# A graph network on one core: the back of a batch as one stream, and as two that overlap

## The chip, the cores and the metric

One core of a Trainium2 chip runs the whole program. The metric is the time of one execution on the device, in microseconds (us); the runs' median is given. The core's engines work side by side, each through its own queue of instructions in the order of the program: TensorE (PE in the profile, its weight loads PEld), VectorE (DVE), ScalarE (ACT), GpSimd (POOL) and SyncE (SP, which here only issues DMAs).

## The reference

16 graphs of 1024 nodes with 64 channels, and a dense weighted adjacency of which some 1.6% is not zero. Four layers, each x = layernorm(x + f(x)):

```python
# layer 0: GCN
x = ln(x + adj @ (x @ w0) + b0)
# layer 1: quantiles over neighbours
adj_ = where(eye, 1, adj)                       # self loops
nb = (adj_ > 0) & ~eye;  m = nb.sum(-1)         # degree
rank = cumsum(nb) - 1
skip = where(m > 10, (m + 1) // 2, 1)
removed = nb & (skip > 1) & mask & ((rank + 1) % skip == 0)
valid = where(removed | removed.T, 0, adj_) > 0
agg = 0.25 * q25 + 0.5 * q50 + 0.25 * q75       # over x[valid neighbours], per channel
x = ln(x + (relu((x + agg) @ W1 + b1) @ W2 + b2) * mask)
# layer 2: three rounds of message passing
h = x @ We
for i in range(3): h = relu(adj @ (h @ Wl[i] + bl[i]))
x = ln(x + (h @ Wp + bp) * mask)
# layer 3
t = adj @ x
x = ln(x + where(t > 0.5, 1, 0))
```

## The kernel before

A batch (one graph) goes through five kinds of work, each written as a Python generator that emits some instructions and yields their cost in planned steps:

- `words_of`: the adjacency comes in eight rows of tiles (`arow`, L488), is transposed on PE, goes to DRAM for later (`adjd`, L604), gives layer 0, and is packed into words of neighbour bits.
- `front` with `listing`: nodes are ranked by their number of neighbours, so that tiles of nodes with similar lists are sorted together. One-hot matrices `perm` (L730, DVE) carry the words into rank order on PE (L735, L736) into PSUM banks "wd", ACT copies them out (L772, L773), and DVE makes lists of neighbours from them (first `bit`, L780). It ends with a table of x1 in DRAM.
- per group of tiles (five groups, `GROUPS`): `gathered` fetches the neighbours' rows by indirect DMAs from POOL (L933; 122 and 7 packed ones a batch), `masked` spoils what does not count (`hits` L981 on DVE, L988 on ACT), `quantiles` runs a sorting network on DVE (L1038) between the buffers `g` and `s`, and `summed` weights the rows on ACT (L1074) and adds them on PE (L1067).
- `back`: the rest of layer 1 and the layers 2 and 3. `to_nodes` brings the sums from rank order back to node order: each of three bf16 `pieces` of the sums is multiplied on PE (L1122) with one-hot matrices `ones_at`, which ACT makes in two operations of 1024 columns (L1117, L1118; in the last batch five of eight are made by DVE, L1114), into two banks at once. Then x1 is added (L1128), two small matmuls and a `residual` with layernorm give x2; the adjacency is read back (`adjB`, L1271, 4 MB); three layers of matmuls with it (L1339, L1350) and a residual give x3; one more aggregation (`aggregate`, L445), a comparison (L1365) and a layernorm give y, which is stored (L1369).

The order of all instructions is made before the program runs. A heap holds the generators by due time; the earliest emits its next step, and its due time grows by the yielded cost times its stretch. `LENGTHS` are the planned durations of the five groups, 192.06 in sum; `start(q)` is the planned start of group q. `back` is due 1.2 after its batch's last group, polls until all five sums are in and the batch before is `done`, and its stretch is BACK / BACK_STEPS = 178/181. One `back` is emitted before the next begins. A gather is also made to follow the fifth DVE and the fourth ACT instruction before it in this order (`follow`). `words_of` of a batch polls until the batch four before is `done` (`LIVES`), and `front` polls until its words are there.

Rooms: PSUM has eight banks: "mm" 2, "tp" 2, "wd" 2, "ax" 1, "agg" 1. In SBUF the one-hot tiles of all kinds (`nb`, `perm`, `ones_at`, `back_to`) share seven rooms of the tag "onehot", and `s` has two rooms. `ENDS` says in which buffer a sorted row ends (1 is `s`).

## Time and profile before

| | |
|---|---|
| median of 10 runs | 3122.62 us (3117.95 to 3126.34) |
| the profiled execution's own time | 3116.19 us |
| its span, first to last instruction | 3114.4 us |
| granted TensorE clock, mean | 0.878 of full speed |
| start of the second subtraction of pieces (L1107), batches 3 to 11 | 871.2, 1049.1, 1227.2, 1404.6, 1584.4, 1763.1, 1942.0, 2121.9, 2299.0 us |

```
## 2 busy tenths in 40 slices
PE   6534697888979798897969788896978889685777
PEld 5434454545545454554545454554545455343443
DVE  7388998989999999999899899989999999987741
ACT  2344757567676756667576756767575666747531
POOL 0577777777777777777777777777777777777600
```

Each digit of a slice row is the busy share of one of 40 equal slices of the span in tenths (9 is 90% or more). In lines of waits the numbers are the total, the count and the longest, in us. In a timeline a line begins with start and duration, and the bracket says how long the engine was idle before and which instruction ended that. In windows an engine's number is its busy time in the stretch, with the instructions in brackets; the last three are the granted clock, the DMA engines' share and GB/s.

### The profile page before, as it was taken

What the parts mean: (1) busy time and instruction counts of PE and PEld (TensorE: products, weight loads), DVE (VectorE), ACT (ScalarE), POOL (GpSimd) and SP (SyncE); (2) the same over time, 40 slices, a digit from 0 to 9 for tenths busy, and PEclk for the clock granted to TensorE, in tenths of its full rate; (3) what the DMA queues carried; (4) which work ended last, traced back from release to release, by engine and by line L of the source; (5) the groups of instructions that cost most, each with busy time, mean ns of one, the idle gap of its engine ahead of it and who ended that gap; (6) DMA issues with size and microseconds to landing.
All of it is one profiled execution on the core that took longest, in us unless ns stands there. A gap on an engine that the chain in (4) does not pass through costs nothing.

```text
span 3114.4 us, 49256 instructions
## 1 busy us (share of the span) xinstructions
PE 2461.5 (79%) x13893; PEld 1508.2 (48%) x13894; DVE 2708.4 (87%) x7852; ACT 1890.4 (61%) x6153; POOL 2207.5 (71%) x2078
## 2 busy tenths in 40 slices
PE   6534697888979798897969788896978889685777
PEld 5434454545545454554545454554545455343443
DVE  7388998989999999999899899989999999987741
ACT  2344757567676756667576756767575666747531
POOL 0577777777777777777777777777777777777600
PEclk8667798989989898998989899898989899787879
DMA  2433334433243434324343433434333332313110
GB/s 87 112 91 77 72 83 116 103 99 103 72 130 93 117 97 116 90 62 147 77 120 90 116 103 83 113 78 128 90 115 101 102 97 71 84 30 85 22 58 5
DMA packets 169079, 282.74 MB, mean 91 GB/s; under 512 B 99485, under 2 KB 102112, under 8 KB 166880
## 3 DMA queue, kind: packets, MB, share of 16 engines
q1 hardware_dynamic: 67584, 142.01, 13.6%
q0 software_dynamic: 66048, 69.88, 13.6%
q10 hardware_dynamic: 35168, 67.62, 5.9%
q8 instruction: 115, 1.88, 0.3%
q14 instruction: 164, 1.34, 0.1%
HBM read 204.33 MB, written 71.44 MB: 89 GB/s over the span
## 4 chain that ended last, share of the span: by engine, by line
DVE 21%; PE 16%; ACT 8%; DMA 3%; issue 2%; POOL 0%; DVEq 0%; POOLq 0%; ACTq 0%
PE mm L1350 8%; DVE s L1038 6%; DVE g L1038 6%; DMA g<-table,idx 3%; ACT ones_at L1117 2%; PE ax L535 2%; ACT g L988 2%; ACT ones_at L1118 2%; PE mm L445 1%; ACT g L1074 1%; PE pa L1067 1%; DVE top L796 1%; PE mm L1339 1%; DVE cand L800 1%; PE tp L510 1%
## 5 line engine op out<-in xcount | busy, mean ns | idle before, releaser
L933 POOL DMA_INDIRECT g<-table,idx x1952 | 2088.0, 1070 | 704.1 <-DMA g<-table,idx 144.4
L1350 PE MATMUL mm<-adjB,msg 128*128 128x512 f32 x1536 | 753.8, 612 | 9.6 <-ACT msg L1342 9.6
L988 ACT ACTIVATE g<-g,bias 128x64 f32<-128x64 f32 (+9 forms) x2272 | 598.1, 339 | 223.8 <-DVE bias L984 164.6
L1038 DVE TENSOR_TENSOR s<-g 128x384 f32<-128x384 f32 (+8 forms) x1200 | 575.8, 495 | 10.2 <-ACT at L512 0.5
L1038 DVE TENSOR_TENSOR g<-s 128x256 f32<-128x256 f32 (+10 forms) x1040 | 501.5, 500 | 3.7
L1067 PE MATMUL pa<-g,ident 128*128 128x128 f32 (+1 forms) x1600 | 332.2, 328 | 117.3 <-ACT g L1074 115.1
L1074 ACT ACTIVATE g<-g,w 128x64 f32<-128x64 f32 x1552 | 394.0, 336 | 29.0 <-DVE w L1045 28.6
L1067 PEld LDWEIGHTS pa<-g,ident 128*128 128x128 f32 x1600 | 269.3, 219 | 266.1 <-ACT g L1074 186.9
L1350 PEld LDWEIGHTS mm<-adjB,msg 128*128 128x128 f32 x1536 | 265.3, 194 | 200.5 <-issue 176.9
L1122 PE MATMUL mm<-ones_at,pieces 128*64 128x512 bf16 x768 | 217.7, 428 | 130.7 <-ACT ones_at L1118 130.7
L535 PE MATMUL ax<-at,xt 128*64 128x128 f32 x1920 | 271.1, 301 | 0.0
L535 PEld LDWEIGHTS ax<-at,xt 128*64 128x64 f32 x1920 | 241.1, 154 | 57.4 <-issue 54.3
L445 PE MATMUL mm<-adjB,x 128*64 128x512 f32 x512 | 245.4, 613 | 8.9 <-DVE x L482 8.9
L1038 DVE TENSOR_TENSOR g<-g 128x256 f32<-128x256 f32 (+7 forms) x432 | 213.2, 507 | 2.5
L1038 DVE TENSOR_TENSOR g<-g,s 128x256 f32<-128x256 f32 (+5 forms) x512 | 209.3, 414 | 3.2
L1122 PEld LDWEIGHTS <-pieces 128*64 128x64 bf16 x768 | 90.1, 120 | 218.8 <-issue 162.2
L510 PE MATMUL tp<-ident,arow 128*128 128x128 f32 x1024 | 165.5, 291 | 24.8 <-DMA arow<-in_adj_dram 16.3
L1353 ACT ACTIVATE hlT<-mm 128x512 f32<-128x512 f32 x96 | 57.2, 596 | 206.2 <-PE mm L1350 206.2
L510 PEld LDWEIGHTS tp<-ident,arow 128*128 128x128 f32 x1024 | 128.0, 150 | 88.0 <-issue 65.4
L735 PE MATMUL wd<-hi,perm 128*128 128x55 f16 x960 | 84.3, 206 | 108.5 <-DVE perm L730 108.3
L981 DVE TENSOR_SCALAR hits<-g,nself 128x38 f32<-128x38 f32 (+4 forms) x128 | 31.6, 247 | 146.6 <-DMA g<-table,idx 122.7
L1010 ACT ACTIVATE hat<-iota,npos 128x10 f32<-128x10 f16 (+2 forms) x384 | 114.4, 298 | 68.7 <-DVE npos L997 67.6
(228 smaller groups left out, 4030.9 us busy)
## 6 DMA issues: line engine op xcount, KB each, us to landing
arow<-in_adj_dram SPq DMA_DIRECT2D x128, 512.0 KB
adjd<-at ACTq DMA_DIRECT2D x120, 512.0 KB
adjB<-adjd SPq DMA_DIRECT2D x15, 4096.0 KB
g<-table,idx POOLq DMA_INDIRECT x1952
table<-xc ACTq DMA_DIRECT2D x16, 264.0 KB
xt<-in_x_dram SPq DMA_DIRECT2D x16, 256.0 KB
out_dram<-y SPq DMA_DIRECT2D x16, 256.0 KB
stage<-table,packed POOLq DMA_INDIRECT x112
```

The costliest lines, as they stand in the source:

```text
L445: nc.tensor.matmul(pa[:C, :], src[:, m, :], adjT[:, h * TH:(h + 1) * TH, m, :], start=(m == 0), stop=(m == T - 1))
L510: nc.tensor.transpose(pt[:, i * P:(i + 1) * P], a[:, j * P:(j + 1) * P], ident)
L535: nc.tensor.matmul(self.bank[:C, cols], self.xt[:, m + 1, :], at[:, m, :], start=(m == 0), stop=(m == T - 1))
L735: nc.tensor.matmul(pw[:, :hn], ws, hi[:, t, :], start=False, stop=False)
L933: g = nc.gpsimd.indirect_dma_start(out=dst, out_offset=None, in_=st["table"], in_offset=bass.IndirectOffsetOnAxis(ap=index, axis=0))
L988: nc.scalar.activation(v, v, AF.Identity, bias=bias[:m, i, k:k + 1])
L1010: nc.scalar.activation(h, iota[:, lo:lo + kw], AF.Abs, bias=npos[:, i, s:s + 1])
L1038: vector.tensor_tensor(box(bufs[mode >> 1 & 1], d, run, sd, count, tile), box(bufs[mode >> 3], a, run, sa, count, tile), box(bufs[mode >> ...
L1067: nc.tensor.matmul(pa[:, :(e - k) * nt * C], ident, rows_.rearrange("p (k c) -> p k c", c=R)[:, :, :C], start=(j == 0), stop=(j == len(run ...
L1074: nc.scalar.activation(slots(g, bufs[0], lo + r, lo + r + 1)[:, i, 0, :C], slots(g, bufs[at[r]], lo + r, lo + r + 1)[:, i, 0, :C], AF.Iden ...
L1122: nc.tensor.matmul(bank[:C, :], pieces[:, i, s, :], ones_at[:, h * HALF:(h + 1) * HALF], start=(s == 0 and i == 0), stop=False)
L1350: nc.tensor.matmul(pg, msg[:, m, :], adjT[:, h * TH:(h + 1) * TH, m, :], start=(m == 0), stop=(m == T - 1))
```

## The change

The `back` becomes two generators. `back_one` goes to x2, with its own rooms for channels, hidden layer, pieces and layernorm, and one PSUM bank of its own, "one"; the bank comes from "wd", of which one is left, so that the permuted words of a batch lie in one bank (8 x 55 columns) and are copied out at once. `back_two` does the rest; it is due 70 planned units after `back_one`, and waits for x2 of its batch and `done` of the batch before. `back_one` waits for x2 of the batch before, no longer for `done`. So the two of neighbouring batches can stand side by side in the order. Inside `to_nodes` the nodes are done in two halves, one after the other, each with `ones_at` of 512 columns and one bank. "onehot" has six rooms for seven and `s` one for two; the sorting network of 13 ends all rows in `g` (one operation of 256 columns becomes two of 128). Other generators keep their due times; the read of `adjB` stands at the start of `back_two`.

```diff
@@ -51,8 +51,8 @@
 LIVES = 4
 STATE = ("nself", "kept", "minus")
 LENGTHS = (50.06, 35, 54.5, 19.5, 33)
-WORDS, LISTS, BACK = 152.6, 133.2, 178
-WORDS_STEPS, LISTS_STEPS, BACK_STEPS = 82.0, 74.0, 181.0
+WORDS, LISTS, BACK1, BACK2 = 152.6, 133.2, 70.0, 160.0
+WORDS_STEPS, LISTS_STEPS, BACK1_STEPS, BACK2_STEPS = 82.0, 74.0, 67.0, 134.0
 BEFORE = 7.874
 AFTER = 1.2
...
@@ -162,7 +162,7 @@
...
-    13: "1000000000",
+    13: "0000000000",
...
@@ -414,7 +414,10 @@
         return psum("tp", 2)
 
     def psum_wd():
-        return psum("wd", 2)
+        return psum("wd", 1)
+
+    def psum_one():
+        return psum("one", 1)
 
     def psum_ax():
         return psum("ax", 1)
@@ -427,10 +430,10 @@
 
 
 
-    def to_channels(dst, src):
+    def to_channels(dst, src, bank):
 
         for h in range(NH):
-            pt = psum_mm()
+            pt = bank()
             for i in range(TH):
                 nc.tensor.transpose(pt[:C, i * P:(i + 1) * P], src[:, h * TH + i, :], ident)
             yield 1.5
...
@@ -723,18 +726,17 @@
         yield 0.4
 
         hn = W + NEXT
-        pws = [psum_wd() for _ in range(NH)]
-        for pw in pws:
-            nc.tensor.matmul(pw[:, :TH * hn], zeros, iota[:, :TH * hn], start=True, stop=False)
+        pws = psum_wd()[:, :T * hn]
+        nc.tensor.matmul(pws, zeros, iota[:, :T * hn], start=True, stop=False)
         def one_hot(t, perm):
             vector.tensor_scalar(perm, iota, rank[:, t:t + 1], None, op0=ALU.is_equal)
 
         def permuted(t, s, perm):
-            pw = pws[s // TH][:, (s % TH) * hn:]
+            pw = pws[:, s * hn:(s + 1) * hn]
             ws = perm[:, s * P:(s + 1) * P]
-            nc.tensor.matmul(pw[:, :hn], ws, hi[:, t, :], start=False, stop=False)
+            nc.tensor.matmul(pw, ws, hi[:, t, :], start=False, stop=False)
             nc.tensor.matmul(pw[:, :W], ws, lo[:, t, 1:W + 1], start=False,
-                             stop=(t == T - 1 and s % TH == TH - 1))
+                             stop=(t == T - 1 and s == T - 1))
 
         if st["b"] == 0:
...
@@ -766,13 +768,11 @@
                     yield 1.0
             st["permuted"] = True
         for half in halves:
-            for h2 in sorted({s // TH for s in half}):
-                v = pws[h2][:, :TH * hn].rearrange("p (t k) -> p t k", k=hn)
-                ts = slice(h2 * TH, (h2 + 1) * TH)
-                nc.scalar.copy(wd[:, ts, :], v[:, :, :W])
-                nc.scalar.copy(num[:, ts, :], v[:, :, W:])
-                yield 0.8
             ts = slice(half[0], half[-1] + 1)
+            v = pws.rearrange("p (t k) -> p t k", k=hn)[:, ts, :]
+            nc.scalar.copy(wd[:, ts, :], v[:, :, :W])
+            nc.scalar.copy(num[:, ts, :], v[:, :, W:])
+            yield 1.2
             wi = wd[:, ts, :]
             for r in range(ROUNDS):
                 if r + 1 < ROUNDS:
...
@@ -1020,7 +1020,7 @@
         nt = len(tiles)
         while ("hat", g) not in st:
             yield 0.5
-        bufs = st["g", g], srt.tile([P, KMAX * R], F32, tag="y", name="s", bufs=2)
+        bufs = st["g", g], srt.tile([P, KMAX * R], F32, tag="y", name="s", bufs=1)
 
         def box(buf, first, run, step, count, tile):
             v = buf[:, (first * nt + max(tile, 0)) * R:]
...
@@ -1099,7 +1099,7 @@
 
 
         ag = st["ag"]
-        pieces = act.tile([P, S, T, C], BF16, tag="msg", name="pieces")
+        pieces = act.tile([P, S, T, C], BF16, tag="pieces", name="pieces")
         for i in range(S):
             nc.scalar.copy(pieces[:, i], ag)
             yield 0.8
@@ -1107,29 +1107,29 @@
                 vector.tensor_tensor(ag, ag, pieces[:, i], ALU.subtract)
                 yield 0.8
         st["moved"] = True
-        banks = [psum_mm() for _ in range(NH)]
-        for s in range(T):
-            ones_at = tmp.tile([P, N], BF16, tag="onehot", name="ones_at", bufs=7)
-            if st["b"] == B - 1 and s % 3:
-                vector.tensor_scalar(ones_at, iota, st["minus"][:, s:s + 1], 0.0,
-                                        op0=ALU.add, op1=ALU.is_equal)
-            else:
-                nc.scalar.activation(ones_at, iota, AF.Abs, bias=st["minus"][:, s:s + 1])
-                nc.scalar.activation(ones_at, ones_at, AF.Relu, bias=1.0, scale=-1.0)
-            yield 1.9
-            for h, bank in enumerate(banks):
+        for h in range(NH):
+            cols = slice(h * HALF, (h + 1) * HALF)
+            bank = psum_one()
+            for s in range(T):
+                ones_at = tmp.tile([P, HALF], BF16, tag="onehot", name="ones_at", bufs=6)
+                if st["b"] == B - 1 and s % 3:
+                    vector.tensor_scalar(ones_at, iota[:, cols], st["minus"][:, s:s + 1], 0.0,
+                                            op0=ALU.add, op1=ALU.is_equal)
+                else:
+                    nc.scalar.activation(ones_at, iota[:, cols], AF.Abs, bias=st["minus"][:, s:s + 1])
+                    nc.scalar.activation(ones_at, ones_at, AF.Relu, bias=1.0, scale=-1.0)
+                yield 1.0
                 for i in range(S):
-                    nc.tensor.matmul(bank[:C, :], pieces[:, i, s, :],
-                                     ones_at[:, h * HALF:(h + 1) * HALF],
+                    nc.tensor.matmul(bank[:C, :], pieces[:, i, s, :], ones_at,
                                      start=(s == 0 and i == 0), stop=False)
-            yield 1.7
-        for h, bank in enumerate(banks):
+                yield 0.9
             for i in range(TH):
                 nc.tensor.matmul(bank[:C, i * P:(i + 1) * P], st["x1"][:, h * TH + i, :], ident,
                                  start=False, stop=(i == TH - 1))
             yield 1.2
-            nc.scalar.copy(dst[:, h * HALF:(h + 1) * HALF], bank[:C, :])
-        yield 1.0
+            nc.scalar.copy(dst[:, cols], bank[:C, :])
+            yield 0.6
...
@@ -1262,65 +1262,66 @@
         return st
 
 
-    def back(st):
-        b, x1 = st["b"], st["x1"]
-        while "words" in st and (st.get("sums", 0) < len(GROUPS) or "done" not in st["before"]):
+    def residual(src, w_sb, first, base, y, mb, bank, who):
+
+        py = bank()
+        add_bias(py, first, C, T)
+        for t in range(T):
+            nc.tensor.matmul(py[:, t * C:(t + 1) * C], src[:, t * P:(t + 1) * P], w_sb,
+                             start=False, stop=(t == T - 1))
+            if t % 2:
+                yield 1.0
+        yield 1.0
+        u = act.tile([P, T, C], F32, tag="u" + who, name="u")
+        vector.tensor_tensor(u, nodes(py), spread(mb, C), ALU.mult)
+        yield 0.7
+        vector.tensor_tensor(u, u, base, ALU.add)
+        yield 0.7
+        yield from layernorm(u, y, who)
+
+    def node_tile(name, tag, bufs=1):
+        return act.tile([P, T, C], F32, tag=tag, name=name, bufs=bufs)
+
+    def back_one(st):
+        x1 = st["x1"]
+        while "words" in st and (st.get("sums", 0) < len(GROUPS) or "x2" not in st["before"]):
             yield 0.5
+        oT = act.tile([C, N], F32, tag="chan1", name="oT")
+        if "agg" in st:
+            o = act.tile([P, T, C], F32, tag="ua", name="o")
+            vector.tensor_tensor(o, x1, st["agg"], ALU.add)
+            yield 0.7
+            yield from to_channels(oT, o, psum_one)
+        else:
+            yield from to_nodes(oT, st)
+        hT = act.tile([H, N], F32, tag="hT1", name="hT")
+        for h in range(NH):
+            cols = slice(h * HALF, (h + 1) * HALF)
+            ph = psum_one()
+            nc.tensor.matmul(ph, w1_sb, oT[:, cols], start=True, stop=True)
+            yield 1.3
+            nc.scalar.activation(hT[:, cols], ph, AF.Relu, bias=b1_sb)
+            yield 0.7
+        x2 = node_tile("x2", "x2", 2)
+        yield from residual(hT, w2_sb, C, x1, x2, st["mb"], psum_one, "a")
+        st["x2"] = x2
+
+    def back_two(st):
+        b = st["b"]
+        while "words" in st and ("x2" not in st or "done" not in st["before"]):
+            yield 0.5
+        x2 = st["x2"]
         if "adjT" not in st:
             st["adjT"] = big.tile([P, T, T, P], F32, tag="adjB", name="adjB")
             nc.sync.dma_start(st["adjT"], st["adjd"])
             yield LANDING
         adjT = st["adjT"]
-        mb = spread(st["mb"], C)
-
-        def wide_u(name):
-            return act.tile([P, T, C], F32, tag="u", name=name)
-
-        def residual(src, w_sb, first, base, y):
-
-            py = psum_mm()
-            add_bias(py, first, C, T)
-            for t in range(T):
-                nc.tensor.matmul(py[:, t * C:(t + 1) * C], src[:, t * P:(t + 1) * P], w_sb,
-                                 start=False, stop=(t == T - 1))
-                if t % 2:
-                    yield 1.0
-            yield 1.0
-            u = wide_u("u")
-            vector.tensor_tensor(u, nodes(py), mb, ALU.mult)
-            yield 0.7
-            vector.tensor_tensor(u, u, base, ALU.add)
-            yield 0.7
-            yield from layernorm(u, y, "b")
-
-        def node_tile(name, tag):
-            return act.tile([P, T, C], F32, tag=tag, name=name)
 
         def chan(name):
             return act.tile([C, N], F32, tag="chan", name=name)
 
-
-        oT = chan("oT")
-        if "agg" in st:
-            o = wide_u("o")
-            vector.tensor_tensor(o, x1, st["agg"], ALU.add)
-            yield 0.7
-            yield from to_channels(oT, o)
-        else:
-            yield from to_nodes(oT, st)
-        hT = act.tile([H, N], F32, tag="hT", name="hT")
-        for h in range(NH):
-            cols = slice(h * HALF, (h + 1) * HALF)
-            ph = psum_mm()
-            nc.tensor.matmul(ph, w1_sb, oT[:, cols], start=True, stop=True)
-            yield 1.3
-            nc.scalar.activation(hT[:, cols], ph, AF.Relu, bias=b1_sb)
-            yield 0.7
-        x2 = node_tile("x2", "x2")
-        yield from residual(hT, w2_sb, C, x1, x2)
-
         x2T = chan("x2T")
-        yield from to_channels(x2T, x2)
+        yield from to_channels(x2T, x2, psum_mm)
         hT = act.tile([H, N], F32, tag="hT", name="h0T")
         for h in range(NH):
             cols = slice(h * HALF, (h + 1) * HALF)
...
@@ -1353,7 +1354,7 @@
                 nc.scalar.activation(hT[:, cols], pg, AF.Relu)
                 yield 0.7
         x3 = node_tile("x3", "x3")
-        yield from residual(hT, wp_sb, 2 * C, x2, x3)
+        yield from residual(hT, wp_sb, 2 * C, x2, x3, st["mb"], psum_mm, "b")
 
         tT = chan("tT")
         yield from aggregate(tT, adjT, x3, psum_mm)
@@ -1361,10 +1362,10 @@
         for t in range(T):
             nc.tensor.transpose(pt[:, t * C:(t + 1) * C], tT[:, t * P:(t + 1) * P], ident[:C, :C])
         yield 2.0
-        u = wide_u("u3")
+        u = act.tile([P, T, C], F32, tag="ub", name="u3")
         vector.scalar_tensor_tensor(u, nodes(pt), 0.5, x3, op0=ALU.is_gt, op1=ALU.add)
         yield 0.7
-        y = node_tile("y", "x2")
+        y = node_tile("y", "x3")
         yield from layernorm(u, y, "b", mean=True)
         nc.sync.dma_start(one(out, b).rearrange("o (t p) c -> p (o t) c", p=P), y)
         st["done"] = True
@@ -1379,7 +1380,7 @@
     def start(q):
         return (q // G) * period + sum(LENGTHS[:q % G])
 
-    state = [{"b": b, "before": {"done": True}} for b in range(B)]
+    state = [{"b": b, "before": {"done": True, "x2": True}} for b in range(B)]
     for b in range(1, B):
         state[b]["before"] = state[b - 1]
     queue = []
@@ -1393,7 +1394,8 @@
         ready = start(b * G - 2) - BEFORE
         add(ready - LISTS - WORDS, words_of(state[b]), WORDS / WORDS_STEPS)
         add(ready - LISTS - (LEAD if b else EARLY), front(state[b]), LISTS / LISTS_STEPS)
-        add(start((b + 1) * G) + AFTER, back(state[b]), BACK / BACK_STEPS)
+        add(start((b + 1) * G) + AFTER, back_one(state[b]), BACK1 / BACK1_STEPS)
+        add(start((b + 1) * G) + AFTER + BACK1, back_two(state[b]), BACK2 / BACK2_STEPS)
         for g in range(G):
             q = b * G + g
             st = state[b]
```

In the network of 13 the step "14,0,8,0,1,1,-3,1,2,-1" becomes "12,0,8,0,1,0,0,0,1,-1;14,1,5,1,1,0,0,0,1,-1".

## The prediction

> **What bounds the kernel now.** First the page: which engine has no idle time left.
>
> ```profile
> span 3114.4 us, 49256 instructions
> PE 2461.5 (79%) x13893; PEld 1508.2 (48%) x13894; DVE 2708.4 (87%) x7852; ACT 1890.4 (61%) x6153; POOL 2207.5 (71%) x2078
> L933 POOL DMA_INDIRECT g<-table,idx x1952 | 2088.0, 1070 | 704.1 <-DMA g<-table,idx 144.4
> ```
>
> POOL looks idle for 29%, but 1952 + 112 gathers stand on one line, and 704 us of idle stand before the 1952. So next the timeline of POOL at the start of one batch's return to node order.
>
> ```profile
> 98.08 1.10 POOL L933 DMA_INDIRECT g<-table,idx  x1 [94.99 <-ACT lo L611]
> ...
> 878.77 0.95 POOL L933 DMA_INDIRECT g<-table,idx  x1 [0.30 <-DVE s L1038]
> 881.59 1.19 POOL L933 DMA_INDIRECT g<-table,idx  x1 [1.87 <-DVE s L1038]
> 883.09 0.97 POOL L933 DMA_INDIRECT g<-table,idx  x1 [0.30 <-DVE hits L981]
> ```
>
> Every gather is followed by the same 0.30 us, whatever is named as releaser: that is the engine's own pace, not a wait. The first gather starts at 98.1, the last ends at 2946.5: 2848 us / 2064 = 1.380 us each. A batch has 122 + 7 = 129, so 129 x 1.38 = 178.0 us, which is the distance between batches that the windows show (178.5, mean of eight). POOL really waits once a batch, 1.5 us at the place shown; the 14 such gaps sum to 14.6 us above 0.30.
>
> Then the waits, for the engine that comes second.
>
> ```profile
> DVE hits L981 <- DMA g<-table,idx: 122.7, 25, 27.0
> DVE u L1290 <- PE mm L1284: 101.4, 16, 60.5
> PE mm L1122 <- ACT ones_at L1118: 130.7, 96, 8.2
> ```
>
> and one batch, and the first 24.8 us of one return to node order, as windows:
>
> ```profile
> 1404.60:1584.40 179.80, 150.51 (x868) 91.66 (x868) 167.63 (x483) 118.35 (x385) 139.64 (x129) 0.91 0.37 102
> 1404.60:1429.40 24.80, 17.37 (x143) 9.05 (x144) 22.50 (x60) 23.78 (x46) 18.46 (x18) 0.81 0.64 217
> ```
>
> DVE works 167.6 of about 178.5 us. Over eight steady batches (902 to 2330) its waits above 0.15 us sum to 7.7 us a batch: 4.1 for gathers (L981), 1.9 for `bit` behind the copy of wd, 1.6 for u (L1290). So gathers set the pace, and DVE has some 4 us a batch to lose before it sets it. The second window shows ACT at 23.8 of 24.8 in the return to node order, PE at 17.4.
>
> Last the tail, PE and DVE after the last gather:
>
> ```profile
> 2969.62 13.52 PE L445 MATMUL mm<-adjB,x 128*64 128x512 f32 x30
> 2984.31 0.69 DVE L1365 SCALAR_TENSOR_TENSOR u<-mm,x 128x512 f32<-128x512 f32 x1 [3.00 <-PE mm L1362]
> 2985.03 0.20 DVE L1045 TENSOR_REDUCE w<-hat 128x13 f32<-128x39 f32 x1
> 2996.49 12.85 PE L1122 MATMUL mm<-ones_at,pieces 128*64 128x512 bf16 x48 [6.56 <-ACT ones_at L1118]
> 3009.17 1.91 PE L1128 MATMUL mm<-ident,xc 128*64 128x128 f32 x16
> 3011.01 1.98 PE L1315 MATMUL mm<-oT,w_sb 64*128 64x512 f32 x4
> ```
>
> Batch 14's last aggregation (L445) is done before batch 15's sums are; its DVE step (L1365) even holds up `w` of the last group by 3.0 us. From 2996 on batch 15 is alone, and PE's chain sets the end (x2 at 3020.0, y at 3108.4, end 3114.4).
>
> The median of ten runs (3122.62) is 6.4 above the profiled execution's own time (3116.19); the sum is made as a difference on the profile and added to the median.
>
> **The change, part by part.** Planner clocks: a planned period is 192.06, a real one 178.5 (0.93 real for 1 planned). A back starts when the sums are in, planned 9 after its batch's sort (0.5 + 8 x 0.72 + 1.5 + 1.0); call the sort's planned end E. Before: 191 steps x 178/181 = 188, done at the next E + 5. After: back_one 54 x 70/67 = 57, done at E + 66; back_two from E + 71.2, 141 x 160/134 = 168, done at the next E + 47. Its residual to x3 lies at the next E - 3 to + 10, its last aggregation at + 10 to + 36: beside the next batch's back_one.
>
> 1. *POOL*: no gather is added, removed or resized: 0. At best its one wait a batch goes: -14.6 us in all.
>
> 2. *ones_at by halves*, ACT: 16 operations of 1024 columns become 32 of 512. L1117 is 1.133 us at 1024, the same kind at L988 0.339 at 64: 0.827 ns a column, so 0.71 at 512; L1118 1.057 - 0.42 = 0.63. A batch: 16 x 1.34 = 21.4 against 8 x 2.19 = 17.5, +3.9 us. It is spread over 34 x 1.045 x 0.93 = 33 us instead of 26, so ACT is as full as before, only longer; after 33 us ACT has room (118 of 178 in the batch). PE's L1122 count and shape stay (48).
>
> 3. *PE beside the return*: L445's 13.8 us now fall on the stretch where the second window has 17.4 of 24.8 busy. L1122's share thins from 0.49 to 0.39 of the time; 17.4 - 2.5 + 13.8 = 28.7 us in 24.8: PE ends some 4 us late, and ACT, longer full, up to 5. What is late next is DVE's `bit` (behind the copy of wd, behind the permutation matmuls), then ln_v and u of the new streams, and behind these in DVE's queue the sort itself. I take +3 at `bit`, +2 for the layernorms, -1.6 because the u wait of x3's residual (now at 1539, where PE is full) leaves its place: +3.4 against a cover of 4.1 (waits for gathers just shrink). Bounds 0 to +6: with the cover gone +2 us x 13 batches = +26. I take +0.25 x 13 = +3.
>
> 4. *DVE in the stretch from L981 to POOL's wait* (the one stretch where DVE's work lengthens the period): the last layernorm (u, two reductions, two passes, four small: 4.3 us) leaves, x3's residual (two u, one reduction, one pass, four small: 3.4) enters. -0.9 a batch at best (-12 in all, part of the 14.6 of item 1), up to +1 if u waits for PE as it does now. I take 0.
>
> 5. *Six rooms for seven, ones_at allocated twice as often*: in this stretch a room comes round after some 8 us instead of 13; a user holds it about 3 us plus PE's lateness of 4. Cover 1 us; with it gone, perm (L730) waits about that on DVE. Inside item 3's bounds.
>
> 6. *One bank for wd*: a batch loses two ACT copies and one zero matmul (0.5 us ACT, off the path). In batch 0 the first half's copies (L772 at 47.28) ran while PE still permuted the second half (until 49.55), in another bank. If they now wait, DVE starts 2.3 later; it waits 2.37 for ACT at 68.49 (ln_v) anyway. 0, bound +2.3. The Trainium skill speaks to this one ("PSUM — Partial Sum Buffer", "PSUM bank collisions raise a hardware error"): engines are to be kept apart by bank, not by address, disjoint columns included. By it the wait is certain; without it the copies could overlap and even the 2.3 would not arise. No run here shows a collision.
>
> 7. *One s buffer*: all sorts now end in g, so s is used by DVE alone, in order: 0. The 13-network splits one operation of 256 columns (0.34 from start to start) into two of 128 (0.20 each): +0.06 x 16 = 1 us, under the cover of item 3.
>
> 8. *adjB's load* moves from the start of the back to back_two's: 17 steps x 1.19 x 0.93 = 19 us ahead of L1350 instead of 60. Its queue's packets reach 4 MB 11.9 to 13.3 us after the issue: hidden by 6 us. On SP's queue it now stands among the arow loads, which wait for transposes; more than 6 us there would stall PE and be felt as in item 3.
>
> 9. *words_of waits for `done` four batches back*: due at start - 346, `done` now at start - 337, so 9 planned late; `front` polls from start - 206 and words were ready at -215: cover 9, then BEFORE's 7.9. 0.
>
> 10. *Tail*: batch 14's aggregation now stands in PE's order among batch 15's L1122. The 3.0 us at L1365 go: -3.0. L445 with the transposes, 15.4 (2967.0 to 2983.1, less pa), enters between 2990 and 3011; of PE's 6.56 idle us ahead of L1122 only the three steps planned earlier use 2.8: +12.6 net. One bank: h waits for the copy (0.58), the two matmul-relu pairs go in series (0.69 + 0.7): +2.0. The first ones_at is half as long: -0.8. Sum +10.8; bounds +4 (all 6.56 us used, sums 2 us earlier still) to +17 (nothing saved).
>
> Sum: +10.8 + 3 = +14: 3122.6 + 14 = 3137 us.
>
> **The rivals.**
> *A, the forecast*: steady pace kept by POOL, the tail longer: 3122.6 + 4 to + 24, so 3127 to 3147. For it: the 0.30 us before every gather. Against: DVE is only 4 us behind.
> *B, PE and ACT become the pace in the stretch after the sort*: overlap puts both over their time there, DVE stalls at `bit` by more than its cover. Decides from a lateness of about 6 us; +1 to +3 a batch: 3122.6 + 11 + 13 x 2 = 3160 (3147 to 3180). For it: ACT at 23.8 of 24.8. Against: both have room 40 us later.
> *C, faster*: the critical stretch of item 4 gets shorter by 0.9, POOL never waits, and the tail stays at its lower end: 3122.6 - 14.6 + 4 = 3112 (3100 to 3116). The steady gain must beat the tail: more than 1 us a batch. For it: layers spread over more time (PE is at 103.8 of 108 us from 1454 to 1562 now). Against: that stretch hardly sets the pace.
> *D, no change*: C's gain and A's tail cancel, or PE covers more of L445 than I allow: 3116.4 to 3128.9. That the streams do not overlap at all is part of it: then the tail stays.
>
> **How the numbers follow.** A 0.42, B 0.21, C 0.19, D 0.18. A change of 0.2% (6.2 us) is about what can be told from none: 3116.4 and 3128.9. A lies above 3128.9 but for 0.04: slower 0.42 + 0.21 - 0.04 = 0.59, same 0.22, faster 0.19. The likeliest is A at 3137, its own range 3127 to 3147. For 8 in 10: down to 3106 (C's far end left out, 0.08), up to 3168 (B's far end, 0.09).
>
> **What would show it.** Gathers at 1.38 us from start to start, 0.30 before nearly all: right. L445 between L1122 blocks, x2 of batch 15 some 10 us later after the last gather: item 10. A growing DVE wait at L780's `bit` and a vanishing one at L981: item 3, B if L981's is gone. PE waiting for adjB: item 8 wrong. A distance between batches under 177 or over 180 us, or shorter gathers beside the moved work, would make the prediction wrong.

## The result, and the profile after

The changed kernel takes 3238.85 us (median of 8 runs, 3237.18 to 3240.65) against 3121.68 us for the kernel before beside it: 1.0377 times as long, 95% interval 1.0368 to 1.0386. The loss is 117 us, where the forecast had +14 and a range to 3168. Ten of the eighteen runs below (e8, e10, e11 and e6, the same four again with a "b", e14 and e10c) fell on chips that took 3633 to 3682 us for the kernel before, with waits that no event in the trace explains; they are set against the kernel before on the same chip, and no size is taken from them.

The page of the changed kernel: span, busy time of the engines, and the line of the gathers.

```profile
span 3236.7 us, 49529 instructions
PE 2556.0 (79%) x13877; PEld 1581.1 (49%) x13878; DVE 2727.5 (84%) x7873; ACT 1939.3 (60%) x6369; POOL 2215.1 (68%) x2078
...
L933 POOL DMA_INDIRECT g<-table,idx x1952 | 2089.7, 1071 | 806.7 <-issue 131.5
```

A gather still takes 1071 ns, and the busy time of each engine grew by 4% or less (5% for TensorE's weight loads). What grew is the idle time ahead of the gathers (704.1 to 806.7 us). From the first gather to the last the pitch went from 1.3802 to 1.4349 us: over 2063 steps that is +112.9. The tail, from the last gather's end to the end of the span, went from 167.9 to 178.6: +10.7. The first gather starts 1.3 earlier. The sum, 122.3, is the difference of the two spans. So the tail came out at the size forecast, and the loss lies in the steady part: the distance between batches, by the second subtraction of pieces (L1107), went from 178.3 to 187.6 us (mean of ten). POOL no longer sets it: its idle time beyond 0.31 us per gather went from 1.1 to 10.0 us a batch.

VectorE's waits in the changed kernel (total, count, longest, in us):

```profile
DVE u L1366 <- PE mm L1363: 131.6, 16, 17.4
DVE hits L981 <- DMA g<-table,idx: 82.1, 18, 27.0
...
DVE u L1276 <- PE one L1270: 56.8, 16, 10.9
DVE deg L670 <- ACT lo L614: 27.5, 12, 3.5
```

In steady batches (means of ten, here and below) these are 7.4, 1.5, 2.8 and 2.5 us a batch; all waits above 0.15 us together went from 7.5 to 15.0. The wait at `bit` (1.9 before) is gone: VectorE stops earlier in its order, at u (L1366), the step that compares and adds in the *previous* batch's layer 3, and comes to `bit` when ScalarE has already copied wd. The first 30 us of a return to node order, before and after, as windows (busy us of PE, PEld, DVE, ACT, POOL, then granted clock):

```profile
1404.60:1434.60 30.00, 22.57 (x170) 12.09 (x171) 27.66 (x70) 28.02 (x58) 22.45 (x22) 0.84 0.55 184
```

```profile
1450.70:1480.70 30.00, 28.79 (x180) 12.52 (x179) 22.29 (x54) 23.08 (x52) 23.10 (x23) 0.94 0.17 28
```

TensorE went from 22.6 to 28.8 of 30: full. ScalarE was full (28.0) and now is not, though it has more to do; it stands, that is, it is idle because the next operation in its order has to wait. Its timeline shows where (start, duration, and in the bracket the idle time before and who ended it):

```profile
1459.99 0.33 ACT L988 ACTIVATE g<-g,bias 128x64 f32<-128x64 f32 x1
1462.93 0.58 ACT L451 COPY tT<-mm 64x512 f32<-64x512 f32 x1 [2.61 <-PE mm L448]
...
1467.91 0.63 ACT L1120 ACTIVATE ones_at<-ones_at 128x512 bf16<-128x512 bf16 x1
1471.58 0.58 ACT L1130 COPY oT<-one 64x512 f32<-64x512 f32 x1 [3.04 <-PE one L1127]
...
1483.11 0.46 ACT L773 COPY wd<-wd 128x384 f32<-128x384 f32 x1
```

Twice in one return ScalarE stands in its order for a bank that TensorE fills late: once for the aggregation of x3, once for the first half of the nodes. 5.65 us go there, and the `ones_at` behind them come that much later; behind the second stand TensorE waits 0.47 us for one in turn. On the other two engines, at the same time:

```profile
1470.51 1.04 PE L1127 MATMUL one<-ident,xc 128*64 128x128 f32 x8
1471.38 1.88 PE L448 MATMUL mm<-adjB,x 128*64 128x512 f32 x4
...
1473.73 0.81 PE L1123 MATMUL one<-ones_at,pieces 128*64 128x512 bf16 x3 [0.47 <-ACT ones_at L1120]
...
1477.40 0.81 PE L1123 MATMUL one<-ones_at,pieces 128*64 128x512 bf16 x3
1478.14 0.71 PE L1363 MATMUL mm<-ident,tT 64*128 64x64 f32 x8
```

```profile
1470.50 1.10 DVE L1038 TENSOR_TENSOR s<-g,s 128x256 f32<-128x256 f32 x3
1478.89 0.69 DVE L1366 SCALAR_TENSOR_TENSOR u<-mm,x 128x512 f32<-128x512 f32 x1 [7.29 <-PE mm L1363]
...
1484.85 0.35 DVE L780 TENSOR_SCALAR bit<-wd 128x384 int32<-128x384 int32 x1
```

VectorE is through with its own work at 20.9 us after the second subtraction (1450.7) and waits until TensorE is through L1363 at 28.1; the rest of the sort stands behind u.

In the tail, the aggregation of batch 14 stands between the L1123 of batch 15's return, as forecast.

```profile
3097.03 7.44 PE L448 MATMUL mm<-adjB,x 128*64 128x512 f32 x10 [3.04 <-DVE x L485]
3104.31 0.81 PE L1123 MATMUL one<-ones_at,pieces 128*64 128x512 bf16 x3
3104.96 1.88 PE L448 MATMUL mm<-adjB,x 128*64 128x512 f32 x4
```

The last second subtraction and the first matmuls on x2, before and after:

```profile
2992.95 0.69 DVE L1107 TENSOR_TENSOR ag<-ag,pieces 128x512 f32<-128x512 f32 x1 [0.68 <-ACT pieces L1104]
3020.03 1.92 PE L435 MATMUL mm<-ident,x 128*64 128x128 f32 x8 [4.79 <-DVE x L482]
```

```profile
3098.27 0.69 DVE L1107 TENSOR_TENSOR ag<-ag,pieces 128x512 f32<-128x512 f32 x1 [0.69 <-ACT pieces L1104]
3142.66 1.91 PE L438 MATMUL mm<-ident,x 128*64 128x128 f32 x8 [4.79 <-DVE x L485]
```

The last gather ends at 2946.5 before and at 3058.0 after. The sums therefore come 6.2 us sooner behind it (40.3 us for 46.5), and the way from there to x2 is 17.3 us longer (44.4 for 27.1).

### The profile page after: what moved, and what is told of

The parts are those of the page before. It is cut to its first block, busy times and chain, and to the rows that moved or that the text cites. A ratio compares the mean times of both kernels' runs of the same rounds, so it can differ in the third digit from the quotient of the medians.

```text
span 3236.7 us, 49529 instructions
## 1 busy us (share of the span) xinstructions
PE 2556.0 (79%) x13877; PEld 1581.1 (49%) x13878; DVE 2727.5 (84%) x7873; ACT 1939.3 (60%) x6369; POOL 2215.1 (68%) x2078
## 4 chain that ended last, share of the span: by engine, by line
DVE 45%; PE 32%; ACT 13%; DMA 6%; issue 3%; POOL 1%; DVEq 0%; ACTq 0%; SPq 0%; POOLq 0%
DVE g L1038 15%; DVE s L1038 13%; PE mm L1351 8%; PE mm L448 6%; DMA g<-table,idx 5%; PE ax L538 3%; PE pa L1067 3%; PE one L1123 3%; ACT g L988 3%; DVE top L796 2%; ACT ones_at L1119 2%; ACT ones_at L1120 2%; DVE cand L800 2%; ACT g L1074 2%; DVE nb L600 1%
## 5 line engine op out<-in xcount | busy, mean ns | idle before, releaser
L933 POOL DMA_INDIRECT g<-table,idx x1952 | 2089.7, 1071 | 806.7 <-issue 131.5
L1351 PE MATMUL mm<-adjB,msg 128*128 128x512 f32 x1536 | 769.8, 614 | 5.2 <-ACT msg L1343 5.2
L448 PE MATMUL mm<-adjB,x 128*64 128x512 f32 x512 | 286.3, 663 | 51.2 <-DVE x L485 51.2
L1123 PE MATMUL one<-ones_at,pieces 128*64 128x512 bf16 x768 | 225.0, 406 | 90.9 <-ACT ones_at L1120 88.5
L538 PE MATMUL ax<-at,xt 128*64 128x128 f32 x1920 | 287.8, 314 | 0.0
L538 PEld LDWEIGHTS ax<-at,xt 128*64 128x64 f32 x1920 | 255.9, 161 | 58.7 <-issue 57.7
L513 PE MATMUL tp<-ident,arow 128*128 128x128 f32 x1024 | 184.4, 316 | 54.4 <-ACT at L515 29.5
L1123 PEld LDWEIGHTS <-pieces 128*64 128x64 bf16 x768 | 86.7, 114 | 258.8 <-issue 222.8
L513 PEld LDWEIGHTS tp<-ident,arow 128*128 128x128 f32 x1024 | 142.5, 165 | 137.9 <-issue 74.7
L515 ACT COPY at<-tp 128x512 f32<-128x512 f32 x240 | 137.8, 575 | 68.2 <-PE tp L513 67.6
L1119 ACT ACTIVATE ones_at<-iota,minus 128x512 bf16<-128x512 f16 x246 | 174.1, 708 | 0.0
L1120 ACT ACTIVATE ones_at<-ones_at 128x512 bf16<-128x512 bf16 x246 | 154.9, 630 | 7.8
```

The source lines that it names most:

```text
L448: nc.tensor.matmul(pa[:C, :], src[:, m, :], adjT[:, h * TH:(h + 1) * TH, m, :], start=(m == 0), stop=(m == T - 1))
L513: nc.tensor.transpose(pt[:, i * P:(i + 1) * P], a[:, j * P:(j + 1) * P], ident)
L538: nc.tensor.matmul(self.bank[:C, cols], self.xt[:, m + 1, :], at[:, m, :], start=(m == 0), stop=(m == T - 1))
L933: g = nc.gpsimd.indirect_dma_start(out=dst, out_offset=None, in_=st["table"], in_offset=bass.IndirectOffsetOnAxis(ap=index, axis=0))
L1119: nc.scalar.activation(ones_at, iota[:, cols], AF.Abs, bias=st["minus"][:, s:s + 1])
L1120: nc.scalar.activation(ones_at, ones_at, AF.Relu, bias=1.0, scale=-1.0)
```

## The experiments

Beside the time stand two measures from each timeline: the time from the second subtraction to the start of `bit`, and the distance between batches (means of ten). The theories: **T1**, TensorE's crowd, the aggregation of the batch before beside the return; **R1**, the return by halves on ScalarE; **R2**, the rooms; **R3**, the one bank "one" of the first stream. T2 to T5 were formed on the way: T2 and T3 divide R1 into the price of the added operations and that of the copy in the middle, T4 says that each of TensorE and ScalarE alone is over the limit, T5 that the return by halves and the second stream add up.

| kernel | median us | ratio to before (95%) | to `bit`, us | batch distance, us |
|---|---|---|---|---|
| before | 3121.68 | 1 | 24.6 | 178.3 |
| e1 rooms alone | 3118.53 | 0.9998 (0.9988 to 1.0007) | 24.5 | 178.9 |
| e8c split operations alone | 3144.41 | 1.0053 (1.0032 to 1.0073) | 28.0 | 180.8 |
| e2 return by halves alone | 3197.87 | 1.0261 (1.0237 to 1.0284) | 30.1 | 185.0 |
| after | 3238.85 | 1.0377 (1.0368 to 1.0386) | 33.9 | 187.6 |
| e3 streams planned apart | 3245.59 | 1.0403 (1.0385 to 1.0420) | 29.6 | 188.9 |
| e5 u later | 3208.21 | 1.0256 (1.0236 to 1.0276) | 42.9 | 185.4 |
| e4 short aggregation | 3185.54 | 1.0212 (1.0195 to 1.0229) | 31.2 | 184.3 |
| e6c no second operation | 3201.46 | 1.0235 (1.0216 to 1.0254) | 31.9 | 184.3 |
| e13 both cuts | 3157.53 | 1.0093 (1.0071 to 1.0116) | 25.7 | 182.2 |

Each ratio is to the kernel before on the same chip (3119.52 us beside e1 to e4, 3129.68 beside e5, e6c, e8c and e13). A late `bit` goes with a longer distance except in e3, where other waits add to it, and in e5, whose edit moves `bit` itself.

**e1, the rooms.** In the kernel before:

```diff
-            nb = tmp.tile([P, T, P], F16, tag="onehot", name="nb", bufs=7)
+            nb = tmp.tile([P, T, P], F16, tag="onehot", name="nb", bufs=6)
...
-        return psum("wd", 2)
+        return psum("wd", 1)
...
-        bufs = st["g", g], srt.tile([P, KMAX * R], F32, tag="y", name="s", bufs=2)
+        bufs = st["g", g], srt.tile([P, KMAX * R], F32, tag="y", name="s", bufs=1)
```

with all "onehot" tiles in six rooms, the network of 13 and the permutation into one bank, as in the change.

> The kernel before with the change's rooms alone: six onehot tiles for seven, one s buffer for two with the changed network of 13, one wd bank for two. The back half stays one stream and the return goes by node tiles as before. T1 (TensorE has more work beside the return than the stretch holds, and VectorE's queue stops at u, L1366): the rooms are covered, 3112 to 3135 us, DVE's wait at bit below 8 us in the whole span more than before. R2 (the rooms set the new pace): at least half of the loss of 117 us is here, 3180 to 3240 us, with waits on buffers of onehot or wd in front of DVE.

The time doesn't change: 0.9998. R2 falls. One wait did arise, in batch 0, where ScalarE copies the first half of the permuted words; the kernel before and e1:

```profile
47.28 0.32 ACT L772 COPY wd<-wd 128x192 f32<-128x192 f32 x1 [12.13 <-PE wd L736]
```

```profile
47.82 0.32 ACT L770 COPY wd<-wd 128x192 f32<-128x192 f32 x1 [14.04 <-PE wd L735]
```

Before, TensorE was still permuting the second half, until 49.55. In e1 the copy starts when the last permutation has ended, at 47.79; that is only 0.5 us later, since the permutation itself had ended 1.8 us earlier than before.

**e2, the return by halves**, in the kernel before, in its banks "mm" and its one stream:

```diff
-        for s in range(T):
-            ones_at = tmp.tile([P, N], BF16, tag="onehot", name="ones_at", bufs=7)
+        for h in range(NH):
+            cols = slice(h * HALF, (h + 1) * HALF)
+            bank = psum_mm()
+            for s in range(T):
+                ones_at = tmp.tile([P, HALF], BF16, tag="onehot", name="ones_at", bufs=7)
...
+            nc.scalar.copy(dst[:, cols], bank[:C, :])
```

> The kernel before with the return by halves of the nodes alone (sixteen pairs of ScalarE operations of 512 columns for eight of 1024), in its old banks and in one stream. T1: TensorE had 22 of 30 us in the return before, so the halves alone don't fill it; ScalarE's 3.9 us a batch are its only price, and at most that much comes through: 3122 to 3165 us. R1 (the halves on ScalarE, not TensorE's crowd, make the return late): 3180 to 3240 us, 4 to 7.5 us a batch.

The loss is 2.6%, without any second stream. Its ScalarE and VectorE show where:

```profile
1447.56 0.63 ACT L1120 ACTIVATE ones_at<-ones_at 128x512 bf16<-128x512 bf16 x1
1451.02 0.58 ACT L1130 COPY oT<-mm 64x512 f32<-64x512 f32 x1 [2.83 <-PE mm L1127]
```

```profile
1463.69 0.36 DVE L780 TENSOR_SCALAR bit<-wd 128x384 int32<-128x384 int32 x1 [4.93 <-ACT wd L772]
```

ScalarE goes from one `ones_at` to the next without a gap until the first half's copy; there it stands for 2.83 us, in a stretch that it fills. VectorE waits for the copy of wd behind it. T1 as the whole cause falls.

**e3, the two streams planned apart**, in the changed kernel:

```diff
-WORDS, LISTS, BACK1, BACK2 = 152.6, 133.2, 70.0, 160.0
+WORDS, LISTS, BACK1, BACK2 = 152.6, 133.2, 60.0, 132.0
```

> The changed kernel with the planned lengths of the two streams set to 60 and 132 us for 70 and 160, so that the second stream of a batch is planned to end near the next batch's first stream's start and the aggregation of x3 comes ahead of the return. Rooms, halves, the single bank stay. T1: the crowd on TensorE in the return goes, the wait at u (L1366) of 131.6 us falls below 30, and 70 to 115 of the lost 117 us come back: 3125 to 3170 us. R1, R2, R3 (halves, rooms, single bank): all of these are still there, so it stays above 3200 us.

The wait at L1366 fell as T1 had it (131.6 to 22.2 us); the time did not fall. VectorE's waits:

```profile
DVE u L1276 <- PE mm L1270: 109.5, 14, 61.0
DVE bit L780 <- ACT wd L773: 90.2, 15, 6.2
DVE u L1276 <- PE one L1270: 88.8, 16, 19.8
```

`bit` now waits as in e2, and the residuals' u (L1276) wait for TensorE in both streams, 7.8 us a batch, where the changed kernel has 2.8 there. The time lies where R1 to R3 had it. The place of a stall is not its cause.

**e4, less work on TensorE beside the return**, in the changed kernel:

```diff
             for m in range(T):
-                nc.tensor.matmul(pa[:C, :], src[:, m, :], adjT[:, h * TH:(h + 1) * TH, m, :],
-                                 start=(m == 0), stop=(m == T - 1))
+                if m in (0, T - 1):
+                    nc.tensor.matmul(pa[:C, :], src[:, m, :], adjT[:, h * TH:(h + 1) * TH, m, :],
+                                     start=(m == 0), stop=(m == T - 1))
                 yield 1.3
```

> The changed kernel with 2 of the 8 matmuls of each half in aggregate (6 of 8 node tiles are left out of the neighbour sums); the order, the planned lengths and all else stay. T1: some 11 us of TensorE's 28.7 beside the return go, the stall at u (L1366) falls from 131.6 us to below 30, 3120 to 3165 us. R1, R2, R3: TensorE's amount of work is not the cause, above 3200 us with the stall at u still above 90 us.

The result lies between the two: 1.65% comes back, and u still waits 84.4 us. In the window TensorE has room, and VectorE is still not busy throughout:

```profile
1434.77:1464.77 30.00, 22.55 (x161) 10.84 (x160) 25.00 (x62) 25.83 (x59) 23.10 (x23) 0.83 0.17 28
```

TensorE now waits 10.4 us a batch for `ones_at` (5.2 in the changed kernel).

**e8, e10, e11, e6, and again as b.** e8: each `ones_at` in two pairs of 512, return by node tiles. e10: e2 with the first half's copy behind the third `ones_at` of the second half. e11: e2 without the second ScalarE operation. e6: the same in the changed kernel.

```diff
-                    nc.scalar.activation(ones_at, ones_at, AF.Relu, bias=1.0, scale=-1.0)
```

> The kernel before, with each ones_at written as two ScalarE pairs of 512 columns in place of one pair of 1024; return by node tiles, one copy of each bank at the end, as before. It adds only ScalarE's price of the halves: 0.71 + 0.63 us per half against 1.15 + 1.05 or so per whole, some 3.9 us a batch. In e2 the return by halves cost 78 us, 5.9 us a batch. T2 (ScalarE is full in the return, the added operations come through one to one, less the 2 to 4 us that VectorE waits on gathers anyway): 3145 to 3180 us. T3 (the cost is the drain in the middle: ScalarE stands 2.83 us for the copy of the first half at 1451.02 of e2 while TensorE ends that half, and TensorE then stands for the next ones_at): 3115 to 3135 us.

> e2 (the kernel before with the return by halves) with the copy of the first half's bank moved behind the third ones_at of the second half, so that ScalarE doesn't stand for TensorE in the middle. The added operations stay. T2: the wait of 2.8 us per batch goes, 3.9 us of operations stay, 3140 to 3175 us. T3: all is back but some, 3115 to 3140 us. If the middle copy is nothing: 3190 to 3205 us.

> e2 without the second ScalarE operation of each half of ones_at (the matrix keeps the distances, not the ones, so the returned sums differ); TensorE's and VectorE's work stays. Takes 15 or 16 x 0.63 = 10 us of ScalarE out of each return. T2 and T3 (ScalarE sets the return's length): VectorE's wait at bit (96 us) goes below 20, 3112 to 3135 us. If TensorE set the return's length instead: 3180 us and above.

> The changed kernel without the second ScalarE operation of each half of ones_at (the returned sums differ, as in the run beside it). T1 (TensorE's own work fills the return of the two streams: 28.7 of 30 us): little comes back, 3195 to 3235 us, with the stall at u (L1366) still above 80 us. T2 (ScalarE's operations set the return's length here too): 3115 to 3150 us. Both in part: between.

> The kernel of e8 on another chip, since the kernel before took 3682 us on the chip of e8, e10, e11 and e6 and its engines stood there without a cause that the trace names. The expectations of e8 stay: T2 (ScalarE is full in the return; 0.707 + 0.630 us for each half against 1.134 + 1.057 us for each whole is 8 x 0.48 = 3.9 us a batch, less what VectorE waits on gathers anyway): 3145 to 3180 us. T3 (the drain in the middle of e2 is the cost): 3115 to 3135 us.

> The kernel of e10 on another chip. The expectations of e10 stay, beside e2's 3198: T2 3140 to 3175 us, T3 3115 to 3140 us, the middle copy costs nothing 3190 to 3205 us.

> The kernel of e11 on another chip (return by halves in the kernel before, without the second ScalarE operation, so that the matrix keeps distances). The expectations of e11 stay: T2 and T3 3112 to 3135 us with VectorE's wait at bit below 20 us; if TensorE set the return's length, 3180 us and above.

> The kernel of e6 on another chip (the changed kernel without the second ScalarE operation of ones_at). The expectations of e6 stay: T1 (TensorE's own work fills the return of the two streams) 3195 to 3235 us with the stall at u (L1366, a line earlier here) above 80 us; T2 (ScalarE's operations set it) 3115 to 3150 us.

On these chips the ratios were 0.9981 and 1.0021 for e8, 1.0151 and 1.0121 for e10, 1.0111 and 1.0133 for e11, 1.0146 and 1.0028 for e6. Neither e2 nor the changed kernel ran there, and e6's two ratios lie 1.2% apart, so none of the expectations is decided by them.

**e6c, less work on ScalarE**, on a chip with the kernel before at 3129.68 us:

> The kernel of e6 on a third chip (the changed kernel without the second ScalarE operation of ones_at). What the traces have shown since: from the second subtraction to the start of bit it is 24.64 us in the kernel before, 30.14 in e2, 33.93 in the changed kernel, 31.19 in e4, and the batch distance follows these shifts. T4 (two queues are over the 20.8 us at which VectorE comes to u, each by itself: TensorE's run to L1363 without a gap, 28.1 us, and ScalarE's operations and stands up to the wd copy, 32.2 us; one alone gives little back): 3205 to 3238 us, the wait at u stays above 90 us. T2 (ScalarE's operations alone): 3115 to 3150 us.

1.42% comes back, and u still waits 114.2 us. The time is just under T4's bounds, and far above T2's. ScalarE is down to 17 of 30 us, and TensorE fills the stretch by itself:

```profile
1440.68:1470.68 30.00, 29.54 (x186) 12.82 (x185) 23.69 (x59) 17.25 (x44) 23.16 (x22) 0.96 0.16 28
```

**e13, both cuts:**

> The changed kernel with both cuts: 2 of 8 matmuls in each half of aggregate (6 of 8 node tiles left out of the neighbour sums) and no second ScalarE operation of ones_at. T4: each alone leaves the other queue as the limit (e4 gave 52 us back), both together give back nearly all, 3115 to 3145 us, with the waits at u (L1366) and bit together below 3 us a batch. T1 alone (TensorE) with e4 as its whole effect: 3175 to 3190 us as in e4.

2.84% comes back, close to the sum of the two (1.65 + 1.42). The waits at u and `bit` went as T4 had it, but the time is above its 3145 us, and "one alone gives little" was wrong: the two prices add. A reading that fits, and was not tested by itself, is that the two queues hand to each other, so that each cut shortens the same chain. The window shows the stretch when neither is late: VectorE is busy throughout.

```profile
1424.92:1454.92 30.00, 23.41 (x176) 12.11 (x174) 29.58 (x75) 21.92 (x59) 23.40 (x22) 0.90 0.18 28
```

In steady batches u at L1366 waits 0.1 us and `bit` not at all. What is left of the loss is 0.93%. VectorE's waits for gathers are 7.5 us a batch, and the mean gather takes 1084 ns for 1068 in the kernel before: over 2064 gathers that is some 32 us, as much as the 28 us that are left. Why they are longer stays open. The one bank "one" (R3) was not tried alone, but e13 keeps it, so it costs 0.93% at most there.

**e5, u later in VectorE's order**, in the changed kernel:

```diff
-        yield 2.0
+        yield 12.0
         u = act.tile([P, T, C], F32, tag="ub", name="u3")
```

> The changed kernel with u (L1366) placed 10 planned us later in VectorE's order. T1 (the stall is VectorE's order at u alone): the 7.3 us a batch shrink to below 2, 3140 to 3185 us. T4 (ScalarE's copy of wd ends at 33.7 us behind the second subtraction in the changed kernel, where bit stands now, so the wait moves from u to bit): 3215 to 3245 us, and the trace shows VectorE's wait of 5 to 8 us a batch at bit.

```profile
DVE bit L780 <- ACT wd L773: 97.7, 15, 8.2
DVE hits L981 <- DMA g<-table,idx: 94.5, 19, 27.1
```

1.21% comes back, less than T1 and a little more than T4 expected; the wait moved from u to `bit`, 6.6 us a batch, as T4 had it. The edit is not clean: `done` comes later too, and `bit` moved back to 42.9 us; that the one comes of the other was not tried.

**e8c, the operations alone:**

```diff
-                nc.scalar.activation(ones_at, iota, AF.Abs, bias=st["minus"][:, s:s + 1])
-                nc.scalar.activation(ones_at, ones_at, AF.Relu, bias=1.0, scale=-1.0)
+                for h in range(NH):
+                    cols = slice(h * HALF, (h + 1) * HALF)
+                    nc.scalar.activation(ones_at[:, cols], iota[:, cols], AF.Abs,
+                                         bias=st["minus"][:, s:s + 1])
+                    nc.scalar.activation(ones_at[:, cols], ones_at[:, cols], AF.Relu, bias=1.0, scale=-1.0)
```

> The kernel of e8 on a third chip (the kernel before, each ones_at written as two pairs of 512 columns, return by node tiles). T2: 3.9 us of ScalarE in a full stretch come through, bit starts 3 to 4 us later than the 24.6 of before, 3145 to 3180 us. T3 (the drain in the middle is the cost of e2): 3115 to 3135 us.

`bit` starts 3.35 us later, as T2 had it, and 2.5 us a batch come through: 0.53% of e2's 2.61%, just under T2's bounds. Most of the price of the halves is therefore not in the operations. The standing of ScalarE ahead of the copy of wd grew from 1.5 to 4.4 us a return in e2, in e8c not at all; that the copy in the middle is the whole rest is argued from this, not shown. Part of the rest is elsewhere: in e2 the mean gather takes 1078 ns for 1068 before, some 1.5 of the 6.7 us a batch.

e8c also tests the cover of the prediction, the 4.1 us that VectorE waits for gathers. A `bit` 3.35 us late should have vanished in it. The waits for gathers shrank by 1.9 us a batch only, and POOL's idle time beyond 0.31 us per gather grew by 2.3. The program ties the two: each gather follows the fifth VectorE instruction before it, so a late VectorE makes the gathers late too. That this tie is the reason fits the numbers; no run leaves it out.

**e14, the changed kernel with the return by node tiles**, the second half of the nodes on partitions 64 to 127 of the one bank, and **e10c**:

```diff
+        both = psum_one()
+        banks = [both[h * C:(h + 1) * C, :] for h in range(NH)]
+        for s in range(T):
+            ones_at = tmp.tile([P, N], BF16, tag="onehot", name="ones_at", bufs=6)
```

> The changed kernel with the return by node tiles again (ones_at of 1024 columns, one ScalarE pair per node tile, both copies at the end). The one bank holds both halves of the nodes, the second on partitions 64 to 127. The two streams, the rooms and all else stay. T5 (the loss is the sum of the return by halves, which cost 2.6 % alone in e2, and of the second stream beside it, some 1.1 %): 3150 to 3175 us. T1 (TensorE's crowd is the cause by itself, whatever the return's shape): 3200 to 3238 us. T4 (each queue alone is over the limit): 3200 to 3225 us, as in e6c.

> The kernel of e10 on another chip: e2 with the copy of the first half's bank moved behind the third ones_at of the second half, the added ScalarE operations stay. e8c has shown that the operations alone cost 0.5 %, e2 is at 2.6 %. If the stand of ScalarE in the middle (2.8 us a batch) is the rest: ratio to before 1.005 to 1.014. If the order by halves costs in another way: 1.020 to 1.028.

The ratios are 1.0223 (1.0176 to 1.0269) for e14 and 1.0136 (1.0087 to 1.0185) for e10c, both on a chip with the kernel before at 3667.5 us. e10c lies in the range that its expectation gives to the stand in the middle, but e2 didn't run on that chip. e14 has no halves and still loses 2.2% there, with 10 us a batch of waits at u (L1367 in it). On the other chips the halves alone are enough for 2.61% and the changed kernel loses 3.77%; how its loss divides between halves and second stream, and whether the two simply add up, is not settled.

## Why the prediction was wrong

The steps that failed are items 2 and 3: how late the return makes VectorE, and the cover that was to take it up. They came to +0.25 us a batch; measured, it is +9.3.

- **Item 2, ones_at by halves.** The sizes were right (708 and 630 ns measured, 0.71 and 0.63 estimated). The place was not: "ACT is as full as before, only longer" gave the +3.9 us a batch no price of its own, and item 3 let the cover take up what came of it at `bit`, though the prediction's own window showed ScalarE at 23.8 of 24.8 us with VectorE's `bit` behind its queue, waiting already. e8c shows 2.5 us a batch, some +17 us in all. The Trainium skill ("ScalarE: Activation LUTs", "What ACT_TABLE_LOAD costs") gives about 280 ns + 0.833 ns a column for an operation whose bias is read from a [128,1] operand, one value for each partition; by that page the estimate is 707 ns at 512 columns, and the 708 measured agree.
- **Not in the prediction at all: the copy in the middle.** A return by halves puts a wait for TensorE into ScalarE's order while eight `ones_at` are still to come: 2.8 us in e2, 3.0 in the changed kernel. e2 as a whole, operations and copy, is +5.5 us at `bit` and +78 us.
- **Item 3, TensorE beside the return: the mechanism right, the size wrong, the place too.** 28.7 us of work were forecast for a stretch of 24.8; measured, TensorE is busy for 28.8 of the first 30. But the 4 us of lateness were counted against the 24.8 us at which VectorE had come to `bit`. VectorE's order now has u (L1366) ahead of `bit`, and VectorE is there after 20.9 us; TensorE is through L1363 at 28.1, so VectorE waits 7.3 us. The plan hides this: by it u stands 27 units behind the second subtraction (aggregation up to E + 36, then 2.0 x 160/134; the sums in at E + 9, then three steps of 0.8 x 70/67), which is 25 us at 0.93, and VectorE runs through this stretch in 0.78 of the plan. The term was +0.25 x 13 = +3 us; the steady part as a whole came to +112.9, the growth of the gathers' pitch.
- **Its cover.** 4.1 us of waits for gathers were to take it up; they gave 2.0 (4.0 to 2.0 us a batch), and in e8c, where less than the cover was asked of them, 1.9. By these numbers they are not free time.
- **Item 1**: gathers unchanged, right (1070 to 1071 ns); "POOL sets the pace" held before the change only, and e8c's 3.35 us already ended it.
- **Items 5, 6, 7**, rooms, one bank, one s buffer: 0 forecast, 0 by e1. The wait at batch 0, with its bound of +2.3 us, did arise in e1 and cost 0.5 us at `bit`; e1's first gather starts at 95.9 us all the same, 2.2 earlier than before. Item 6 took the wait as certain by the rule of the Trainium skill ("PSUM — Partial Sum Buffer", "PSUM bank collisions raise a hardware error") that two engines are to be kept apart in one bank. The copy does wait, but e1 doesn't separate this rule from the order that the program itself sets.
- **Item 8**, the load of adjB hidden: right, no wait of TensorE on it. **Item 4**, VectorE's shorter stretch: not to be seen beside this loss. **Item 9**: `deg` (L670) waits 2.5 us a batch behind ScalarE's `lo`; whether that comes of the late ScalarE or of the later `done` was not tried alone.
- **Item 10, the tail**: +10.8 forecast, +10.7 measured, and this is in part luck. The sums were to come 3.0 us sooner and came 6.2 sooner; the way from there to x2 was to be 13.8 us longer (12.6 + 2.0 - 0.8) and is 17.3 longer. The two errors offset each other. The lower bound was given as +4, where its own terms make +5.
- **The rivals.** B named what happened, both engines over their time in the return and VectorE standing, though at `bit` and not at u, and from a lateness of some 6 us; it is 7.3. It had +1 to +3 us a batch; it is +9.3.

## What to carry to other kernels

Before work is put beside a stretch, add up every engine's queue in that stretch, and set against it the time in which the *waiting* engine gets there, from the trace and not from the plan. An engine's waits need not be cover: where the program makes what it waits for follow it, as here, count on part of them at most (here 2.0 of 4.1 us). Splitting a loop in two puts its closing copy into the middle of a queue that runs in order, and the engine can stand there while it has work to do. A wait that goes away when work is moved need not show in the time; e3 lost 109 us of one wait and was no faster.

## What the runs showed of the hardware

In these windows TensorE's granted clock is higher where TensorE is busier. The first 30 us of a return in e2 and in the changed kernel, the first 5 apart (the clock is the third number from the end, ahead of the DMA share):

```profile
1433.54:1438.54 5.00, 3.20 (x22) 1.65 (x22) 4.93 (x14) 4.20 (x8) 3.78 (x5) 0.50 0.94 402
1438.54:1463.54 25.00, 16.66 (x126) 8.60 (x126) 17.43 (x47) 21.77 (x51) 17.22 (x17) 0.84 0.50 156
```

```profile
1450.70:1455.70 5.00, 5.00 (x25) 1.84 (x24) 4.93 (x14) 4.20 (x8) 3.89 (x4) 0.64 0.12 20
1455.70:1480.70 25.00, 23.79 (x157) 10.68 (x156) 17.36 (x41) 18.88 (x44) 19.21 (x20) 1.00 0.17 29
```

In e2, TensorE is busy for 19.9 of the 30 us, and its clock is 0.50 at first and 0.84 on average behind that; in the changed kernel it is busy for 28.8, and the clock is 0.64 and then 1.00. The windows of 30 us above lie in the same order: 22.6 us busy at 0.83 (e4) and at 0.84 (before), 23.4 at 0.90 (e13), 28.8 at 0.94 (after), 29.5 at 0.96 (e6c). The DMAs don't make this order: e4 and the kernel before have the same clock at DMA shares of 0.17 and 0.55. The durations of the 48 multiplications with `ones_at`, which overlap, add up to 23.2 us a batch in e2, 20.5 in the kernel before and 19.4 in the changed kernel: a crowd on TensorE gives a little of its price back. The Trainium skill ("TensorE: Matmul & The Clock Gate", "Part 1: The HAM clock gate") has the same: half rate is the rest state, and sustained work releases it.
